# Graph kernel: block transposes on VectorE and a DMA round trip in place of TensorE transposes

## The chip, the cores and the metric

The kernel runs on one core of one Trainium2 chip. The metric is the device time of one execution in microseconds (us), lower is better. Faster or slower needs a difference of over 2%.

## The reference, cut to what matters

128 independent graphs, each with 128 nodes of 512 features and a 128x128 adjacency matrix. Everything is fp32.

```python
h = relu(layernorm(x))
H = (adj != 0);  w = adj[:, 0, :]
S = H diag(1/colsum(H)) H^T;   Dn = 1 / (H @ w)            # per graph
z = relu(Dn * S @ (h @ W1.T) + b1)                          # hidden width 1024
y = Dn * S @ (layernorm(z) * gamma + beta) @ W2.T + b2      # back to 512
x = x + (y + h)
h = relu(layernorm(x))
agg = (adj @ h) / max(rowsum(adj), 1e-6)
out = x + relu(concat(h, agg) @ W.T)
```

## The kernel before

Graphs go through a software pipeline: each step of the outer loop runs one stage of each of some fourteen graphs, and a scheduler then fixes the order in which each engine executes the instructions ("the built order" below). In the traces here an engine keeps to its order, so an instruction whose input is late holds up all behind it: in one run below, 3.78 us per graph. A tile pool hands out a fixed number of buffers in rotation (`bufs`).

A product on TensorE is written `matmul(out, a, b)` and gives the transpose of a times b, so the left operand must lie transposed. The results land in banks of a memory called PSUM, from which ScalarE or VectorE copies ("evicts") them. Four things are transposed on TensorE: two of the adjacency (`pt`), the normalised hidden layer R (`pnt`, eight 128x128 blocks) and the second layer's input h3 (`ph3`, four):

```python
    def norm_and_transposes(b):
        ...
        pt = bank("pt")
        nc.tensor.transpose(pt[:, 0:P], H.pop(b), ident)
        nc.tensor.transpose(pt[:, P : 2 * P], AN.pop(b), ident)
        ...
    def node_matrix(b):
        ps = psmall.tile([P, P + 1], FP, tag="ps_s", name="ps_s")      # one PSUM bank
        nc.tensor.matmul(ps, HT.pop(b), SB.pop(b), start=True, stop=True)
        S[b] = pool.tile([P, P], FP, tag="s", name="s", bufs=10)
        nc.scalar.activation(S[b], ps[:, :P], AF.Copy)
        dn = pool.tile([P, 1], FP, tag="dn", name="dn")
        nc.vector.tensor_copy(dn, ps[:, P : P + 1])
        ...
    def inner_transposes(b):
        n = R.pop(b)
        NT[b] = pool.tile([P, KH, P], FP, tag="nt", name="nt")
        for j in range(KH // 4):
            pt = bank("pnt")
            for i in range(4):
                k = 4 * j + i
                nc.tensor.transpose(pt[:, i * P : (i + 1) * P], n[:, k * P : (k + 1) * P], ident)
            ... # PSUM -> NT, one half by ScalarE, one by VectorE
    def conv2_weights(b):
        n = NT.pop(b)
        pg = bank("pg")
        for k in range(KH):
            nc.tensor.matmul(pg, n[:, k, :], w2[:, k, :], start=(k == 0), stop=(k == KH - 1))
        ...
    def conv2_nodes(b):
        py = bank("py")
        nc.tensor.matmul(py, S.pop(b), G.pop(b), start=True, stop=True)
        ... # VectorE evicts py into x1
```

SyncE issues three DMAs per graph: adj, x and out.

Of the kernel before, what the change touches and what calls it, by code (L numbers as in the profile page):

```python
# [8 lines left out]
FP = mybir.dt.float32  # L9
AF = mybir.ActivationFunctionType  # L10
ALU = mybir.AluOpType
AX = mybir.AxisListType
PSUM = bass.MemoryType.PSUM

# [6 lines left out]
def gnn_kernel(  # L21
# [26 lines left out]
    pool = ctx.enter_context(tc.tile_pool(name="pool", bufs=2))  # L48
    psum = ctx.enter_context(tc.tile_pool(name="psum", bufs=7, space=PSUM))
# [5 lines left out]
    X, ADJ = {}, {}  # L55

    def load(b):
        X[b] = pool.tile([P, D], FP, tag="x", name="x_t", bufs=5)
        ADJ[b] = pool.tile([P, P], FP, tag="adj", name="adj_t", bufs=4)
        nc.sync.dma_start(out=ADJ[b], in_=adj[b])  # L60
        nc.sync.dma_start(out=X[b], in_=x[b])


    row0 = const.tile([N, P], FP, name="row0")
# [6 lines left out]
    nc.scalar.dma_start(out=row0, in_=adj[:, 0, :])  # L71
    nc.scalar.dma_start(out=w1, in_=w1t.rearrange("(k p) h -> p k h", p=P))
    nc.scalar.dma_start(out=b1_bc, in_=b1.partition_broadcast(P))
    nc.gpsimd.dma_start(out=gb[:, 0, :], in_=gamma)
    nc.gpsimd.dma_start(out=gb[:, 1, :], in_=beta)
    nc.gpsimd.dma_start(out=w2, in_=w2t.rearrange("(k p) o -> p k o", p=P))
    nc.gpsimd.dma_start(out=b2_bc, in_=b2.partition_broadcast(P))
    nc.gpsimd.dma_start(out=w3, in_=wt.rearrange("(k p) o -> p k o", p=P))

    ident = const.tile([P, P], FP, name="ident")  # L80
    make_identity(nc, ident)
    eps = const.tile([P, 1], FP, name="eps")
    nc.vector.memset(eps, EPS_LN)


    wcol = const.tile([P, N], FP, name="wcol")
    pw = bank("pw")
    nc.tensor.transpose(pw[:, :N], row0, ident[:N, :N])
    nc.vector.tensor_copy(wcol, pw[:, :N])
# [37 lines left out]
    H, AN, HT, ANT, SB, S, DN = ({} for _ in range(7))  # L127
    H0, XB, Z1, R, NT, G, X1, H3, H3T, AGT = ({} for _ in range(10))

    def stats_and_incidence(b):  # L130
        ST1[b] = ln_stats(X[b], D, "l1")
        a = ADJ.pop(b)
        H[b] = pool.tile([P, P], FP, tag="h_inc", name="h_inc", bufs=3)
        nc.vector.tensor_scalar(H[b], a, 0.0, None, ALU.not_equal)
        deg = pool.tile([P, 1], FP, tag="deg", name="deg")
        nc.vector.tensor_reduce(deg, a, AX.X, ALU.add)
        rdeg = pool.tile([P, 1], FP, tag="rdeg", name="rdeg")
        nc.vector.tensor_scalar(rdeg, deg, EPS_DEG, None, ALU.max)
        nc.vector.reciprocal(rdeg, rdeg)
        AN[b] = pool.tile([P, P], FP, tag="an", name="an", bufs=3)  # L140
        nc.vector.tensor_scalar(AN[b], a, rdeg, None, ALU.mult)  # L141

    def norm_and_transposes(b):
        H0[b] = pool.tile([P, D], FP, tag="h0", name="h0", bufs=4)
        ln_relu(H0[b], X[b], *ST1.pop(b), "l1")
        pt = bank("pt")
        nc.tensor.transpose(pt[:, 0:P], H.pop(b), ident)  # L147
        nc.tensor.transpose(pt[:, P : 2 * P], AN.pop(b), ident)  # L148
        HT[b] = pool.tile([P, P], FP, tag="ht", name="ht", bufs=3)
        ANT[b] = pool.tile([P, P], FP, tag="ant", name="ant", bufs=14)  # L150
        cnt = pool.tile([P, 1], FP, tag="cnt", name="cnt")
        nc.scalar.activation(HT[b], pt[:, 0:P], AF.Copy, accum_out=cnt)
        nc.scalar.activation(ANT[b], pt[:, P : 2 * P], AF.Copy)

        be = pool.tile([P, 1], FP, tag="be", name="be")
        nc.vector.tensor_scalar(be, cnt, 1.0, None, ALU.max)
        nc.vector.reciprocal(be, be)
        SB[b] = pool.tile([P, P + 1], FP, tag="sb", name="sb", bufs=3)
        nc.vector.tensor_scalar(SB[b][:, :P], HT[b], be, None, ALU.mult)
        nc.vector.tensor_copy(SB[b][:, P : P + 1], wcol[:, b : b + 1])  # L160
        XB[b] = pool.tile([P, D], FP, tag="xb", name="xb", bufs=10)
        nc.gpsimd.tensor_tensor(XB[b], X.pop(b), H0[b], ALU.add)  # L162


    def node_matrix(b):
        ps = psmall.tile([P, P + 1], FP, tag="ps_s", name="ps_s")
        nc.tensor.matmul(ps, HT.pop(b), SB.pop(b), start=True, stop=True)  # L167
        S[b] = pool.tile([P, P], FP, tag="s", name="s", bufs=10)
        nc.scalar.activation(S[b], ps[:, :P], AF.Copy)  # L169
        dn = pool.tile([P, 1], FP, tag="dn", name="dn")  # L170
        nc.vector.tensor_copy(dn, ps[:, P : P + 1])
        inv = pool.tile([P, 1], FP, tag="inv", name="inv")
        nc.vector.tensor_scalar(inv, dn, TINY, None, ALU.max)
        nc.vector.reciprocal(inv, inv)
        DN[b] = pool.tile([P, 1], FP, tag="dinv", name="dinv", bufs=10)
        nc.vector.scalar_tensor_tensor(DN[b], dn, 0.0, inv, ALU.is_gt, ALU.mult)  # L176
# [10 lines left out]
    def conv1_weights(b):  # L187
        z = Z1.pop(b)
        R[b] = pool.tile([P, DH], FP, tag="r", name="r", bufs=5)
        for j in range(DH // 512):  # L190
            cols = slice(j * 512, (j + 1) * 512)
            po = bank("po1")
            for k in range(KD):
                nc.tensor.matmul(po, z[:, k, :], w1[:, k, cols], start=(k == 0), stop=(k == KD - 1))  # L194
            nc.vector.scalar_tensor_tensor(R[b][:, cols], po, DN[b], b1_bc[:, cols], ALU.mult, ALU.add)  # L195
        nc.scalar.activation(R[b], R[b], AF.Relu)  # L196
# [10 lines left out]
    def inner_transposes(b):  # L207
        n = R.pop(b)
        NT[b] = pool.tile([P, KH, P], FP, tag="nt", name="nt")
        for j in range(KH // 4):  # L210
            pt = bank("pnt")
            for i in range(4):
                k = 4 * j + i
                nc.tensor.transpose(pt[:, i * P : (i + 1) * P], n[:, k * P : (k + 1) * P], ident)  # L214
            dst = NT[b][:, 4 * j : 4 * j + 4, :].rearrange("p k c -> p (k c)")
            if j % 2:
                nc.scalar.activation(dst, pt, AF.Copy)  # L217
            else:
                nc.vector.tensor_copy(dst, pt)
# [18 lines left out]
    def norm_layer1(b):  # L238
        H3[b] = pool.tile([P, D], FP, tag="h3", name="h3")
        ln_relu(H3[b], X1[b], *ST3.pop(b), "l3")  # L240

    def aggregate(b):
        h, an = H3.pop(b), ANT.pop(b)
        pt = bank("ph3")
        pa = bank("pag")
        for k in range(KD):
            nc.tensor.transpose(pt[:, k * P : (k + 1) * P], h[:, k * P : (k + 1) * P], ident)  # L247
# [3 lines left out]
        H3T[b] = pool.tile([P, KD, P], FP, tag="h3t", name="h3t")  # L251
        AGT[b] = pool.tile([P, KD, P], FP, tag="agt", name="agt")
        nc.vector.tensor_copy(H3T[b].rearrange("p k c -> p (k c)"), pt)
        nc.scalar.activation(AGT[b].rearrange("p k c -> p (k c)"), pa, AF.Copy)

    def finish(b):
        halves = (H3T.pop(b), AGT.pop(b))
        po = bank("po2")
        for k in range(2 * KD):
            nc.tensor.matmul(po, halves[k // KD][:, k % KD, :], w3[:, k, :],  # L260
                             start=(k == 0), stop=(k == 2 * KD - 1))
# [15 lines left out]
        (ahead + 8, conv2_weights),  # L277
        (ahead + 9, conv2_nodes),
        (ahead + 10, norm_layer1),
        (ahead + 11, aggregate),  # L280
        (ahead + 12, finish),
# [43 lines left out]
```

## Time and profile before

| | before |
|---|---|
| time, median of 3 runs | 3257.86 us (3257.32 to 3258.47) |
| period, from one `out` to the next | 24.99 us |
| first `out` issued | 162.7 us after the start |
| DMA engines busy | 8% from 40 us on |
| SyncE | 3 DMAs per graph, 0.45 to 0.47 us each when back to back |

The view of SyncE's waits, by the line that waited and what ended the wait; the columns are us in total, times, longest:

```profile
SPq L60 <- DVE rdeg L138: 1983.2, 121, 17.4
SPq L264 <- DVE o L263: 752.5, 128, 24.6
```

SyncE stands still for over 2700 of 3256 us. L264 is the store of `out`; its 752.5 us are time in which SyncE had nothing to do but wait for a result.

### The profile page before, as it was taken

The numbers are of one execution on the slowest core, as the hardware profiler recorded it, in microseconds if no ns is written. First come the engines' busy times: TensorE is split into PE (matmuls) and PEld (weight loads), VectorE is DVE, ScalarE is ACT, GpSimd is POOL, SyncE is SP. The second block draws the span as 40 slices with busy tenths as digits, with TensorE's granted clock in tenths as the row PEclk, the third lists the DMA queues.
The fourth block names the chain that finished last, engine by engine and source line by source line (L and its number), as shares of the span: only waits on it lengthen the run. The fifth ranks groups of instructions, "written<-read, shape, count | busy, mean of one in ns | idle before, by whom it ended". The sixth has DMA issues, their size and how long they took to land.

```text
span 3256.2 us, 29056 instructions
## 1 busy us (share of the span) xinstructions
PE 3212.4 (99%) x10513; PEld 1662.9 (51%) x10513; DVE 1598.9 (49%) x4236; ACT 720.3 (22%) x1665; POOL 335.2 (10%) x267
## 2 busy tenths in 40 slices
PE   5999999999999999999999999999999999999999
PEld 2555555555555555555555555555555555555554
DVE  6644454455445544554455445544554455444332
ACT  2222222222222222222222222222222222222211
POOL 2100010011001100110010001000100010001000
PEclk9999999999999999999999999999999999999999
DMA  3000000000000000000000000000000000000000
GB/s 137 24 26 22 23 26 26 22 23 28 23 22 23 29 22 23 23 29 22 22 23 29 22 22 24 28 22 22 26 26 22 22 26 26 22 22 10 13 10 23
DMA packets 57456, 84.53 MB, mean 26 GB/s; under 512 B 6304, under 2 KB 22816, under 8 KB 57312
## 3 DMA queue, kind: packets, MB, share of 16 engines
q1 hardware_dynamic: 55296, 75.52, 7.1%
q0 software_dynamic: 1200, 4.46, 0.4%
q10 hardware_dynamic: 816, 2.69, 0.2%
q8 instruction: 82, 1.34, 0.2%
q14 instruction: 62, 0.51, 0.0%
HBM read 49.09 MB, written 33.55 MB: 25 GB/s over the span
## 4 chain that ended last, share of the span: by engine, by line
PE 98%; DMA 1%; DVE 0%; ACT 0%; SPq 0%; issue 0%; ACTq 0%
PE po L194 27%; PE po L260 27%; PE pg L225 27%; PE pz L182 4%; PE pag L249 3%; PE pnt L214 3%; PE py L233 3%; PE ph L247 2%; PE ps_s L167 1%; PE pt L147 0%; PE pt L148 0%; DMA x_t<-in_x_dram 0%; DMA adj_t<-in_adj_dram 0%; PE pc L100 0%; DVE an L141 0%; DVE rs L119 0%
## 5 line engine op out<-in xcount | busy, mean ns | idle before, releaser
L194 PE MATMUL po<-w,z 128*128 128x512 f32 x2048 | 901.4, 593 | 1.3 <-ACT z L185 1.3
L225 PE MATMUL pg<-w,nt 128*128 128x512 f32 x2048 | 899.8, 592 | 0.0
L225 PEld LDWEIGHTS pg<-w,nt 128*128 128x128 f32 x2048 | 389.0, 190 | 489.3 <-issue 475.7
L194 PEld LDWEIGHTS po<-w,z 128*128 128x128 f32 x2048 | 379.7, 190 | 431.6 <-issue 429.3
L195 DVE SCALAR_TENSOR_TENSOR r<-po,dinv,b_bc 128x512 f32<-128x512 f32 x256 | 192.2, 751 | 713.0 <-PE po L194 713.0
L260 PE MATMUL po<-w,h3t 128*128 128x512 f32 x1024 | 460.8, 593 | 0.1
L260 PE MATMUL po<-w,agt 128*128 128x512 f32 x1024 | 460.3, 592 | 0.0
L162 POOL TENSOR_TENSOR xb<-x_t,h 128x512 f32<-128x512 f32 x128 | 169.3, 1323 | 2689.0 <-ACT h L124 2689.0
L227 DVE TENSOR_TENSOR g<-pg,c 128x512 f32<-128x512 f32 x128 | 88.5, 691 | 543.6 <-PE pg L225 543.6
L196 ACT ACTIVATE r<-r 128x1024 f32<-128x1024 f32 x128 | 135.3, 1057 | 876.6 <-DVE r L195 876.6
L260 PEld LDWEIGHTS po<-w,agt 128*128 128x128 f32 x1024 | 194.6, 190 | 244.9 <-issue 244.9
L113 ACT ACTIVATE sd<-mv,eps 128x1 f32<-128x1 f32 x384 | 113.9, 298 | 837.4 <-DVE mv L111 824.7
L260 PEld LDWEIGHTS po<-w,h3t 128*128 128x128 f32 x1024 | 184.8, 190 | 185.6 <-issue 184.8
L217 ACT ACTIVATE nt<-pnt 128x512 f32<-128x512 f32 x128 | 76.4, 597 | 543.9 <-PE pnt L214 543.9
L205 DVE TENSOR_SCALAR r<-r,mv,l2rs 128x1024 f32<-128x1024 f32 x128 | 194.5, 1520 | 0.4
L182 PEld LDWEIGHTS pz<-s,h 128*128 128x128 f32 x1024 | 135.2, 193 | 61.4 <-issue 60.7
L109 DVE BATCH_NORM_STATS2 st<-r 128x6 f32<-128x512 f32 x256 | 162.8, 676 | 7.2 <-ACT r L196 7.2
L229 POOL TENSOR_TENSOR xb<-xb,b_bc 128x512 f32<-128x512 f32 x128 | 161.7, 1265 | 9.7
L214 PEld LDWEIGHTS pnt<-ident,r 128*128 128x128 f32 x1024 | 119.9, 141 | 66.9 <-issue 66.9
L176 DVE SCALAR_TENSOR_TENSOR dinv<-dn,inv 128x1 f32<-128x1 f32 x128 | 151.3, 1182 | 0.0
L235 DVE SCALAR_TENSOR_TENSOR x<-py,dinv,xb 128x512 f32<-128x512 f32 x128 | 96.1, 750 | 88.1 <-PE py L233 88.1
L182 PE MATMUL pz<-s,h 128*128 128x128 f32 x1024 | 136.0, 276 | 0.4 <-ACT s L169 0.4
(63 smaller groups left out, 2316.2 us busy)
## 6 DMA issues: line engine op xcount, KB each, us to landing
x_t<-in_x_dram SPq DMA_DIRECT2D x128, 256.0 KB, 2.7
out_dram<-o SPq DMA_DIRECT2D x128, 256.0 KB, 2.0
adj_t<-in_adj_dram SPq DMA_DIRECT2D x128, 64.0 KB, 1.8
w<-in_w1t_dram ACTq DMA_DIRECT2D x1, 2048.0 KB, 13.2
w<-in_w2t_dram POOLq DMA_DIRECT2D x1, 2048.0 KB, 15.9
w<-in_wt_dram POOLq DMA_DIRECT2D x1, 2048.0 KB, 23.3
b_bc<-in_b_dram ACTq DMA_DIRECT2D x1, 512.0 KB, 7.8
b_bc<-in_b_dram POOLq DMA_DIRECT2D x1, 256.0 KB, 16.9
```

The source lines that it names most:

```text
L109: nc.vector.bn_stats(st[:, i, :], src[:, i * 512 : (i + 1) * 512])
L162: nc.gpsimd.tensor_tensor(XB[b], X.pop(b), H0[b], ALU.add)
L176: nc.vector.scalar_tensor_tensor(DN[b], dn, 0.0, inv, ALU.is_gt, ALU.mult)
L182: nc.tensor.matmul(pz[:, k * P : (k + 1) * P], h[:, k * P : (k + 1) * P], S[b], start=True, stop=True)
L194: nc.tensor.matmul(po, z[:, k, :], w1[:, k, cols], start=(k == 0), stop=(k == KD - 1))
L195: nc.vector.scalar_tensor_tensor(R[b][:, cols], po, DN[b], b1_bc[:, cols], ALU.mult, ALU.add)
L196: nc.scalar.activation(R[b], R[b], AF.Relu)
L205: nc.vector.tensor_scalar(R[b], R[b], mv[:, 0:1], rs, ALU.subtract, ALU.mult)
L214: nc.tensor.transpose(pt[:, i * P : (i + 1) * P], n[:, k * P : (k + 1) * P], ident)
L225: nc.tensor.matmul(pg, n[:, k, :], w2[:, k, :], start=(k == 0), stop=(k == KH - 1))
L229: nc.gpsimd.tensor_tensor(XB[b], XB[b], b2_bc, ALU.add)
L260: nc.tensor.matmul(po, halves[k // KD][:, k % KD, :], w3[:, k, :], start=(k == 0), stop=(k == 2 * KD - 1))
```

## The change

Its intent is to give TensorE's transposes to engines that have time. VectorE transposes each 32x32 block in its place; the tile goes to DRAM and comes back with the blocks at their places, in runs of 32 elements, 128 B. The weights are permuted once so that their loads stay contiguous.

```diff
-        for j in range(KH // 4):
-            pt = bank("pnt")
-            ...  nc.tensor.transpose(pt[...], n[...], ident) ... copies out of PSUM
+        NT[b] = pool.tile([P, KH, P], FP, tag="nt", name="nt", bufs=3)
+        spread_blocks(NT[b], R.pop(b), DH, "n")
...
+    def spread_blocks(dst, src, width, tag):
+        K = width // P
+        t = pool.tile([P, width], FP, tag=tag + "bt", name="bt")
+        nc.vector.transpose(t, src)
+        d = dram.tile([P, width], FP, tag=tag + "d", name="scratch")
+        nc.sync.dma_start(out=d, in_=t)
+        for jj in range(Q):                      # Q = 4, B = 32
+            for i in range(Q):
+                nc.sync.dma_start(
+                    out=dst[B * jj : B * (jj + 1), :, B * i : B * (i + 1)],
+                    in_=d[B * i : B * (i + 1)].rearrange("a (j k b) -> j a k b", j=Q, k=K)[jj],
+                )
...                                              # h3 the same; adj and an by 4 DMAs each:
+    def load_blocks(dst, src):
+        for j in range(Q):
+            nc.sync.dma_start(
+                out=dst[B * j : B * (j + 1), :].rearrange("b (i a) -> b i a", a=B),
+                in_=src.rearrange("(i b) (j a) -> j b i a", b=B, a=B)[j],
+            )
...
-        S[b] = pool.tile([P, P], FP, tag="s", name="s", bufs=10)
+        S[b] = pool.tile([P, P], FP, tag="s", name="s", bufs=11)
```

More of the change, by code (lines that the diff above doesn't have):

```diff
@@ L5 @@
 from concourse import mybir
-from concourse.masks import make_identity
 from concourse._compat import with_exitstack
@@ L13 @@
 PSUM = bass.MemoryType.PSUM
+DRAM = bass.MemoryType.DRAM
 EPS_LN = 1e-5
@@ L48, in gnn_kernel @@
     pool = ctx.enter_context(tc.tile_pool(name="pool", bufs=2))
+    dram = ctx.enter_context(tc.tile_pool(name="dram", bufs=3, space=DRAM))
     psum = ctx.enter_context(tc.tile_pool(name="psum", bufs=7, space=PSUM))
@@ L53, in bank @@
         return psum.tile([P, 512], FP, tag="ps", name=name)
-    X, ADJ = {}, {}
+    X, ADJ, ADJB = {}, {}, {}
+    B = 32
+    Q = P // B
+    def load_blocks(dst, src):
[16 more added lines that the diff above has]
+                )
     def load(b):
@@ L59, in load @@
         ADJ[b] = pool.tile([P, P], FP, tag="adj", name="adj_t", bufs=4)
+        ADJB[b] = pool.tile([P, P], FP, tag="adjb", name="adjb", bufs=4)
         nc.sync.dma_start(out=ADJ[b], in_=adj[b])
+        load_blocks(ADJB[b], adj[b])
         nc.sync.dma_start(out=X[b], in_=x[b])
-    row0 = const.tile([N, P], FP, name="row0")
     w1 = const.tile([P, KD, DH], FP, name="w1")
@@ L70, in gnn_kernel @@
     gb = const.tile([P, 2, KH], FP, name="gb")
-    nc.scalar.dma_start(out=row0, in_=adj[:, 0, :])
     nc.scalar.dma_start(out=w1, in_=w1t.rearrange("(k p) h -> p k h", p=P))
     nc.scalar.dma_start(out=b1_bc, in_=b1.partition_broadcast(P))
-    nc.gpsimd.dma_start(out=gb[:, 0, :], in_=gamma)
-    nc.gpsimd.dma_start(out=gb[:, 1, :], in_=beta)
-    nc.gpsimd.dma_start(out=w2, in_=w2t.rearrange("(k p) o -> p k o", p=P))
+    for jj in range(Q):
+        part = slice(B * jj, B * (jj + 1))
+        for i, v in enumerate((gamma, beta)):
+            src = v.rearrange("(l a) (j h) -> j a h l", a=B, j=Q)[jj]
+            for h in range(2):
+                nc.gpsimd.dma_start(out=gb[part, i, 4 * h : 4 * h + 4], in_=src[:, h, :])
+        nc.gpsimd.dma_start(out=w2[part], in_=w2t.rearrange("(j k a) o -> j a k o", j=Q, a=B)[jj])
     nc.gpsimd.dma_start(out=b2_bc, in_=b2.partition_broadcast(P))
-    nc.gpsimd.dma_start(out=w3, in_=wt.rearrange("(k p) o -> p k o", p=P))
-    ident = const.tile([P, P], FP, name="ident")
-    make_identity(nc, ident)
+    for jj in range(Q):
+        nc.gpsimd.dma_start(out=w3[B * jj : B * (jj + 1), :KD, :],
+                            in_=wt[:D].rearrange("(j k a) o -> j a k o", j=Q, a=B)[jj])
+    nc.gpsimd.dma_start(out=w3[:, KD:, :], in_=wt[D:].rearrange("(k p) o -> p k o", p=P))
     eps = const.tile([P, 1], FP, name="eps")
     nc.vector.memset(eps, EPS_LN)
-    wcol = const.tile([P, N], FP, name="wcol")
-    pw = bank("pw")
-    nc.tensor.transpose(pw[:, :N], row0, ident[:N, :N])
-    nc.vector.tensor_copy(wcol, pw[:, :N])
     betas = const.tile([P, KH, P], FP, name="betas")
@@ L126, in gnn_kernel @@
     ST1, ST2, ST3 = {}, {}, {}
-    H, AN, HT, ANT, SB, S, DN = ({} for _ in range(7))
+    HT, ANB, ANT, SB, S, DN = ({} for _ in range(6))
     H0, XB, Z1, R, NT, G, X1, H3, H3T, AGT = ({} for _ in range(10))
@@ L132, in stats_and_incidence @@
         a = ADJ.pop(b)
-        H[b] = pool.tile([P, P], FP, tag="h_inc", name="h_inc", bufs=3)
-        nc.vector.tensor_scalar(H[b], a, 0.0, None, ALU.not_equal)
         deg = pool.tile([P, 1], FP, tag="deg", name="deg")
@@ L139, in stats_and_incidence @@
         nc.vector.reciprocal(rdeg, rdeg)
-        AN[b] = pool.tile([P, P], FP, tag="an", name="an", bufs=3)
-        nc.vector.tensor_scalar(AN[b], a, rdeg, None, ALU.mult)
-    def norm_and_transposes(b):
-        H0[b] = pool.tile([P, D], FP, tag="h0", name="h0", bufs=4)
-        ln_relu(H0[b], X[b], *ST1.pop(b), "l1")
-        pt = bank("pt")
-        nc.tensor.transpose(pt[:, 0:P], H.pop(b), ident)
-        nc.tensor.transpose(pt[:, P : 2 * P], AN.pop(b), ident)
+        an = pool.tile([P, P], FP, tag="an", name="an")
+        nc.vector.tensor_scalar(an, a, rdeg, None, ALU.mult)
+        d = dram.tile([P, P], FP, tag="and", name="an_scratch")
+        nc.sync.dma_start(out=d, in_=an)
+        ANB[b] = pool.tile([P, P], FP, tag="anb", name="anb")
+        load_blocks(ANB[b], d)
+        at = pool.tile([P, P], FP, tag="adjt", name="adjt")
+        nc.vector.transpose(at, ADJB.pop(b))
         HT[b] = pool.tile([P, P], FP, tag="ht", name="ht", bufs=3)
-        ANT[b] = pool.tile([P, P], FP, tag="ant", name="ant", bufs=14)
         cnt = pool.tile([P, 1], FP, tag="cnt", name="cnt")
-        nc.scalar.activation(HT[b], pt[:, 0:P], AF.Copy, accum_out=cnt)
-        nc.scalar.activation(ANT[b], pt[:, P : 2 * P], AF.Copy)
+        nc.vector.tensor_scalar(HT[b], at, 0.0, None, ALU.not_equal, ALU.add, accum_out=cnt)
         be = pool.tile([P, 1], FP, tag="be", name="be")
@@ L159, in norm_and_transposes @@
         nc.vector.tensor_scalar(SB[b][:, :P], HT[b], be, None, ALU.mult)
-        nc.vector.tensor_copy(SB[b][:, P : P + 1], wcol[:, b : b + 1])
-        XB[b] = pool.tile([P, D], FP, tag="xb", name="xb", bufs=10)
+        nc.vector.tensor_copy(SB[b][:, P : P + 1], at[:, 0:1])
+    def norm_and_transposes(b):
+        H0[b] = pool.tile([P, D], FP, tag="h0", name="h0", bufs=4)
+        ln_relu(H0[b], X[b], *ST1.pop(b), "l1")
+        ANT[b] = pool.tile([P, P], FP, tag="ant", name="ant", bufs=13)
+        nc.vector.transpose(ANT[b], ANB.pop(b))
+        XB[b] = pool.tile([P, D], FP, tag="xb", name="xb", bufs=11)
         nc.gpsimd.tensor_tensor(XB[b], X.pop(b), H0[b], ALU.add)
@@ L174, in node_matrix @@
         nc.vector.reciprocal(inv, inv)
-        DN[b] = pool.tile([P, 1], FP, tag="dinv", name="dinv", bufs=10)
+        DN[b] = pool.tile([P, 1], FP, tag="dinv", name="dinv", bufs=11)
         nc.vector.scalar_tensor_tensor(DN[b], dn, 0.0, inv, ALU.is_gt, ALU.mult)
@@ L188, in conv1_weights @@
         z = Z1.pop(b)
-        R[b] = pool.tile([P, DH], FP, tag="r", name="r", bufs=5)
+        R[b] = pool.tile([P, DH], FP, tag="r", name="r", bufs=4)
         for j in range(DH // 512):
@@ L207, in inner_transposes @@
     def inner_transposes(b):
-        n = R.pop(b)
-        NT[b] = pool.tile([P, KH, P], FP, tag="nt", name="nt")
-        for j in range(KH // 4):
-            pt = bank("pnt")
-            for i in range(4):
-                k = 4 * j + i
-                nc.tensor.transpose(pt[:, i * P : (i + 1) * P], n[:, k * P : (k + 1) * P], ident)
-            dst = NT[b][:, 4 * j : 4 * j + 4, :].rearrange("p k c -> p (k c)")
-            if j % 2:
-                nc.scalar.activation(dst, pt, AF.Copy)
-            else:
-                nc.vector.tensor_copy(dst, pt)
+        NT[b] = pool.tile([P, KH, P], FP, tag="nt", name="nt", bufs=3)
+        spread_blocks(NT[b], R.pop(b), DH, "n")
     def conv2_weights(b):
@@ L238, in norm_layer1 @@
     def norm_layer1(b):
-        H3[b] = pool.tile([P, D], FP, tag="h3", name="h3")
+        H3[b] = pool.tile([P, D], FP, tag="h3", name="h3", bufs=3)
         ln_relu(H3[b], X1[b], *ST3.pop(b), "l3")
+        H3T[b] = pool.tile([P, KD, P], FP, tag="h3t", name="h3t", bufs=4)
+        spread_blocks(H3T[b], H3[b], D, "h")
     def aggregate(b):
         h, an = H3.pop(b), ANT.pop(b)
-        pt = bank("ph3")
         pa = bank("pag")
-        for k in range(KD):
-            nc.tensor.transpose(pt[:, k * P : (k + 1) * P], h[:, k * P : (k + 1) * P], ident)
         for k in range(KD):
@@ L250, in aggregate @@
                              start=True, stop=True)
-        H3T[b] = pool.tile([P, KD, P], FP, tag="h3t", name="h3t")
         AGT[b] = pool.tile([P, KD, P], FP, tag="agt", name="agt")
-        nc.vector.tensor_copy(H3T[b].rearrange("p k c -> p (k c)"), pt)
         nc.scalar.activation(AGT[b].rearrange("p k c -> p (k c)"), pa, AF.Copy)
     def finish(b):
-        halves = (H3T.pop(b), AGT.pop(b))
+        h, g = H3T.pop(b), AGT.pop(b)
         po = bank("po2")
         for k in range(2 * KD):
-            nc.tensor.matmul(po, halves[k // KD][:, k % KD, :], w3[:, k, :],
-                             start=(k == 0), stop=(k == 2 * KD - 1))
+            lhs = h[:, k, :] if k < KD else g[:, k - KD, :]
+            nc.tensor.matmul(po, lhs, w3[:, k, :], start=(k == 0), stop=(k == 2 * KD - 1))
         o = pool.tile([P, D], FP, tag="o", name="o", bufs=3)
@@ L276, in gnn_kernel @@
         (ahead + 7, inner_transposes),
-        (ahead + 8, conv2_weights),
-        (ahead + 9, conv2_nodes),
-        (ahead + 10, norm_layer1),
-        (ahead + 11, aggregate),
-        (ahead + 12, finish),
+        (ahead + 9, conv2_weights),
+        (ahead + 10, conv2_nodes),
+        (ahead + 11, norm_layer1),
+        (ahead + 12, aggregate),
+        (ahead + 13, finish),
     ]
```

## The prediction

> **What bounds the kernel now.** I read the page first (busy shares, then the chain that ended last), then one period of the chain in order of time, then the timeline of the issuing queue and the DMA packets.
>
> ```profile
> PE 3212.4 (99%) x10513; PEld 1662.9 (51%) x10513; DVE 1598.9 (49%) x4236; ACT 720.3 (22%) x1665; POOL 335.2 (10%) x267
> ...
> PE 98%; DMA 1%; DVE 0%; ACT 0%; SPq 0%; issue 0%; ACTq 0%
> ```
>
> TensorE is busy 99% of the span and is 98% of the chain. Nothing else is above half. Busy alone would not settle it, since matmul records overlap, so I read the chain of one period, where each piece stands with its own advance:
>
> ```profile
> 1604.81 6.87 PE po L260 x16
> 1611.68 0.44 PE ph L247 x4
> 1612.12 0.89 PE pag L249 x8
> 1613.01 0.86 PE py L233 x2
> 1613.87 6.87 PE pg L225 x16
> 1620.74 0.87 PE pnt L214 x8
> 1621.61 6.87 PE po L194 x16
> 1628.48 0.89 PE pz L182 x8
> 1629.37 0.22 PE ps_s L167 x2
> 1629.59 0.11 PE pt L147
> 1629.70 0.11 PE pt L148
> 1629.81 6.87 PE po L260 x16
> ```
>
> One graph takes 1629.81 - 1604.81 = 25.00 us, all of it TensorE, with no gap between pieces. 128 graphs make 3200 us; the other 56 us of the 3256 us span are filling, draining and the one-off preparation of the second weights. In the same period VectorE is busy 12.5 us and ScalarE 5.6 us. So time is won here only by taking work from TensorE, until something else needs as long per graph.
>
> **What the Trainium skill says.** "TensorE: Matmul & The Clock Gate", Part 4: PE-mode transpose, gives about 275 ns for a 128x128 transpose in a kernel. The trace has 273 ns for one record, but four of them advance the chain by 0.44 us: 110 ns each, since they overlap. The measurement decides; the gain is counted at 110 ns, not 275.
> "VectorE: DVE Perf Modes", The three transpose paths, says that VectorE transposes 32x32 blocks only, so something else must move the blocks: here the DMA. The trace before has no such transpose.
> "DMA: Bandwidth & Descriptors", Two DMAs through the same engine are not ordered, says that a DMA which reads what another wrote must wait for its semaphore. So each read of a scratch tile stands behind the landing of its write, and the queue issues in order. The trace before has no such pair.
> The same page, Why small descriptors are slow, speaks of a fixed cost per packet. The trace agrees in kind: its packet records have a median of 9 ns for 4 B, 27 ns for 512 B, 84 ns for 2 KB and 159 ns for 4 KB, about 9 ns plus 36 ns per KB. It has no 128 B packet on this queue.
>
> **The change part by part.**
> *Removed from TensorE*, per graph: pnt 0.87, ph 0.44, the two pt 0.22, together 1.53 us. The period falls to 23.47 us; over 128 graphs 196 us, 6.0%. This is all on the path. No matmul is added.
>
> *ScalarE* loses the copies out of PSUM (0.60 + 0.28 + 0.21 + 0.29 = 1.4 us per graph). It was not the bound.
>
> *VectorE* loses two 128x512 copies (0.68 us each) and gains four transposes. An estimate from the trace's statistics instruction, which takes 694 ns for 512 fp32 elements[...], so 160 ns beside the elements: 1.23 us for 1024 elements, 0.69 for 512, 0.29 each for the two of 128. Sum +2.5 - 1.4 = +1.1 us: 13.6 of 23.5 us. It lies beside TensorE.
>
> *The issuing queue* (SyncE) goes from 3 DMAs per graph to 46: adj, 4 adjb, x, an scratch, 4 anb, h scratch, 16 h3t, n scratch, 16 nt, out. How long does an issue take? The trace has runs of back-to-back issues only at the start:
>
> ```profile
> 0.74 0.39 SPq L60 DMA_DIRECT2D adj_t<-in_adj_dram  x1
> 1.19 0.42 SPq L61 DMA_DIRECT2D x_t<-in_x_dram  x1
> 1.66 0.42 SPq L60 DMA_DIRECT2D adj_t<-in_adj_dram  x1
> 2.12 0.43 SPq L61 DMA_DIRECT2D x_t<-in_x_dram  x1
> 2.60 0.73 SPq L60 DMA_DIRECT2D adj_t<-in_adj_dram  x1
> ...
> 14.41 0.33 SPq L60 DMA_DIRECT2D adj_t<-in_adj_dram  x1
> ```
>
> A lone issue takes 0.33 us (the last line); in a run they come every 0.45 to 0.47 us. 46 x 0.47 = 21.6 us. To this comes one stall: in the built order the writes of h, n and an scratch stand together, and the first h3t read waits for the h write. A 256 KB store takes 2.0 us from issue to landing alone; behind x and out (8 packets of 84 ns per engine each, 0.67 us) it should land about 2.7 us after its issue, 1.4 us of which the two other scratch issues and the next slot cover: about 1.3 us of stall. A handful of extra waits (17 ns plus a gap of 45 ns before the issue) make 0.3. Sum: 21.6 + 1.3 + 0.3 = 23.2 us per graph, against 23.47 for TensorE. **The two are equal within my error.**
>
> *The 16 DMA engines*: adjb and anb are 512 pieces of 128 B each, h3t 2048, nt 4096, together 7168, or 448 per engine and graph. The rest per engine: x, out and h scratch 3 x 8 x 84 ns = 2.0 us; n scratch 8 x 159 = 1.3; adj and an 2 x 8 x 27 = 0.4; 46 semaphore packets of 9 ns = 0.4; sum 4.1 us. By the line above a 128 B piece is 13.6 ns, 6.1 us; if it costs as much as a 512 B one, 12.1 us. So 10 to 16 us of 23.5: hidden. It would bind at (23.47 - 4.1) / 448 = 43 ns per piece.
>
> *Latency and buffers.* At most eight of these DMAs are in flight, since each waits for the one eight before it. At 0.47 us this binds only if one takes over 3.8 us to land; adj takes 1.8. In the built order each landed tile is used about two periods after the output that let its cycle start, one stage having been added: a cycle of 20 to 24 us fits in. So I expect no wait for latency, only for throughput.
>
> *Ends.* The identity, whose making held TensorE until 30.7 us, goes away, but the last graph's tiles travel through the scratch: 2.7 us and 16 issues of 0.47, about 10 us. I leave the 56 us as they are.
>
> **The rivals.**
> 1. TensorE stays the bound: 128 x 23.47 + 56 = 3060 us, -6.0%. For it: the sums above stay below 23.47. Against: the issue sum does so by 0.3 us.
> 2. SyncE's issue becomes the bound. If a patterned DMA with 256 pieces issues in 0.52 us, as some at the start do, the sum is 46 x 0.52 + 1.6 = 25.5 us, 3320 us, +2%; at 0.60, 29.2 us, 3794 us. For it: the runs at the start show 0.73 once and 0.58 once. Against: those fell in microseconds in which the DMA engines were over 90% busy with weights, which they will not be.
> 3. The DMA engines become the bound: at 60 ns per piece 448 x 0.060 + 4.1 = 31 us, over 4000 us. For it: nothing this small has been measured here. Against: 512 B take 27 ns and a semaphore write 9.
> 4. The gain is spent on VectorE: at 13.6 of 23.5 us I see no room for this, even with transposes at twice my estimate.
>
> **Range and chances.** The floor is rival 1, 3060, or some 10 us less if the start gets shorter. A mean of the issue bound over 0.45 to 0.50 us per issue gives 22.3 to 24.6 us, and the larger of it and 23.47 averages near 24.0: 128 x 24.0 + 56 = 3128 us. The errors lie upward, as rivals 2 and 3 have no ceiling nearby. Range 3050 to 3500. Faster by over 2% needs a period below (3193 - 56) / 128 = 24.5 us: 0.52. Slower by over 2% needs one above 25.5: 0.29. Between: 0.19.
>
> **What would show each step.** Right: the page still has TensorE at 97% or more, matmul pieces without gaps, and a period of 23.5 us; VectorE near 57%; the DMA share at 45 to 70%. Rival 2: the waits of TensorE end on nt or h3t DMAs, SyncE issues without pause, every 0.5 us or more, and the DMA engines are well below full. Rival 3: the DMA share at 9 tenths in each slice, and h3t or nt reads that land 4 us or more after issue, so that the wait for the DMA eight before binds. The prediction is wrong if an issue of a 256-piece DMA takes clearly over 0.5 us, or a 128 B piece over 43 ns.

## The result, and the profile after

| | before | after |
|---|---|---|
| time, median of 4 runs | 3257.92 us | 3204.07 us (3202.39 to 3207.99) |
| period, mean of 113 steady ones | 25.00 us | 24.65 us |
| first `out` issued | 162.7 us | 182.5 us |
| DMAs issued by SyncE per graph | 3 | 46 |

The ratio is 0.9836, 95% interval 0.9819 to 0.9853: 1.6% less time. Ratios here are the mean time of one kernel's runs over that of the other's of the same rounds, so not quite the ratio of the quoted medians. The page of after, engine shares, the share of the hardware queue at the DMA engines, and the chain that ended last:

```profile
PE 3058.6 (95%) x8720; PEld 1492.6 (47%) x8720; DVE 1623.1 (51%) x4619; ACT 616.2 (19%) x1153; POOL 380.3 (12%) x286
...
q1 hardware_dynamic: 1110016, 302.37, 40.5%
...
PE 65%; SPq 17%; DMA 11%; DVE 4%; issue 3%; ACT 1%; DVEq 0%; POOL 0%
```

TensorE still looks nearly full at 95%, but its share of the chain fell from 98% to 65%. SyncE's issues (SPq) and the DMAs behind them took the rest. The DMA engines are at 40%, nowhere near full. The timeline of SyncE shows one whole cycle (start, duration, what was issued):

```profile
1614.05 0.38 SPq L277 DMA_DIRECT2D out_dram<-o  x1
1614.48 0.95 SPq L74 DMA_DIRECT2D scratch<-bt  x2
1615.48 0.53 SPq L165 DMA_DIRECT2D an_scratch<-an  x1
1619.75 7.43 SPq L77 DMA_DIRECT2D h3t<-scratch  x16
1627.28 7.78 SPq L77 DMA_DIRECT2D nt<-scratch  x16
1635.16 1.82 SPq L63 DMA_DIRECT2D anb<-an_scratch  x4
1637.02 0.43 SPq L86 DMA_DIRECT2D adj_t<-in_adj_dram  x1
1637.49 1.94 SPq L63 DMA_DIRECT2D adjb<-in_adj_dram  x4
1639.53 0.38 SPq L88 DMA_DIRECT2D x_t<-in_x_dram  x1
1640.01 0.38 SPq L277 DMA_DIRECT2D out_dram<-o  x1
```

From `out` to `out` this one takes 25.96 us (24.65 in the mean), and SyncE issues without a pause but for one hole: from 1616.01 to 1619.75, between the scratch writes and the first read of them. In the mean over the steady cycles, the step from an_scratch to the first h3t read is 2.45 us, of which about 0.49 is an ordinary step, so the stall is 2.0 us; the other 45 steps take 22.2 us, 0.493 each. The chain, in order of time (its longest pieces), goes the same way in the next cycle:

```profile
1640.10 0.28 SPq L277
1640.38 0.05 issue
1640.43 3.48 DMA scratch<-bt
1643.98 0.32 SPq L77
1644.30 0.04 issue
1644.34 0.43 SPq L77
...
1650.98 1.85 DMA h3t<-scratch
1652.84 0.09 issue
1652.93 7.11 PE po L274 x16
```

The write of h3 to the scratch lands 3.48 us after its issue. Then the h3t reads follow each other at 0.43 us plus 0.04 to 0.05 of "issue". TensorE starts on the last of them. SyncE's waits say the same:

```profile
SPq L77 <- DMA scratch<-bt: 215.4, 124, 3.7
SPq L277 <- DVE o L276: 33.0, 9, 8.7
```

The wait for the scratch write is new, in nearly every cycle. The wait for `o`, the slack, fell from 752.5 to 33.0 us. SyncE is the bound.

Where the 50 us came from, in the profiled executions: the first `out` came 19.8 us later, 113 steady periods at 24.65 instead of 25.00 us saved 39 us, and the last 14 periods, in which there is nothing left to load, saved 31 us.

### The profile page after: what moved, and what is told of

Its sections match the earlier page's. It is cut to its first block, busy times and chain, and to the rows that moved or that the text cites. A ratio compares the mean times of both kernels' runs of the same rounds, so it can differ in the third digit from the quotient of the medians. Undisturbed runs are those within 1.5% of the kernel's fastest.

```text
span 3206.2 us, 32427 instructions
## 1 busy us (share of the span) xinstructions
PE 3058.6 (95%) x8720; PEld 1492.6 (47%) x8720; DVE 1623.1 (51%) x4619; ACT 616.2 (19%) x1153; POOL 380.3 (12%) x286
## 4 chain that ended last, share of the span: by engine, by line
PE 65%; SPq 17%; DMA 11%; DVE 4%; issue 3%; ACT 1%; DVEq 0%; POOL 0%
PE po L274 25%; PE po L220 16%; PE pg L241 16%; SPq L77 14%; DMA scratch<-bt 5%; PE pag L264 3%; PE py L249 3%; DMA h3t<-scratch 2%; SPq L63 2%; PE pz L208 1%; DMA nt<-scratch 1%; DVE st L133 1%; DVE x L251 1%; DMA anb<-an_scratch 1%; PE ps_s L193 0%
## 5 line engine op out<-in xcount | busy, mean ns | idle before, releaser
L220 PEld LDWEIGHTS po<-w,z 128*128 128x128 f32 x2048 | 391.0, 191 | 497.7 <-issue 479.8
L241 PEld LDWEIGHTS pg<-w,nt 128*128 128x128 f32 x2048 | 380.1, 190 | 440.1 <-issue 438.4
L274 PE MATMUL po<-w,h3t 128*128 128x512 f32 x1024 | 475.9, 608 | 93.1 <-DMA h3t<-scratch 48.8
L276 DVE SCALAR_TENSOR_TENSOR o<-po,x 128x512 f32<-128x512 f32 x128 | 88.5, 691 | 509.6 <-PE po L274 509.6
L267 ACT ACTIVATE agt<-pag 128x512 f32<-128x512 f32 x128 | 76.4, 597 | 787.4 <-PE pag L264 787.4
L245 POOL TENSOR_TENSOR xb<-xb,b_bc 128x512 f32<-128x512 f32 x128 | 200.9, 1571 | 9.7
L72 DVE STREAM_TRANSPOSE bt<-r 128x1024 f32<-128x1024 f32 x128 | 158.0, 1235 | 32.8 <-DMA scratch<-bt 32.7
L264 PEld LDWEIGHTS pag<-ant,h 128*128 128x128 f32 x1024 | 134.4, 192 | 60.8 <-issue 60.8
L264 PE MATMUL pag<-ant,h 128*128 128x128 f32 x1024 | 134.9, 275 | 0.0
```

What stands on the lines that cost most here:

```text
L72: nc.vector.transpose(t, src)
L220: nc.tensor.matmul(po, z[:, k, :], w1[:, k, cols], start=(k == 0), stop=(k == KD - 1))
L245: nc.gpsimd.tensor_tensor(XB[b], XB[b], b2_bc, ALU.add)
L264: nc.tensor.matmul(pa[:, k * P : (k + 1) * P], h[:, k * P : (k + 1) * P], an, start=True, stop=True)
L274: nc.tensor.matmul(po, lhs, w3[:, k, :], start=(k == 0), stop=(k == 2 * KD - 1))
```

## The experiments

Theory A: SyncE's issues, about 0.49 us each, plus the stall behind the scratch write set the period. Theory B: the DMA engines or the 128 B pieces set it. Theory C: only the wait for the round trip does. Each diff is against the changed kernel unless said otherwise; ratios are against the kernel before.

### e_plus4: four more issues

```diff
         nc.sync.dma_start(out=X[b], in_=x[b])
+        for j in range(4):
+            junk = pool.tile([B, B], FP, tag="junk", name="junk", bufs=8)
+            nc.sync.dma_start(out=junk, in_=adj[b, B * j : B * (j + 1), :B])
```

> The changed kernel with four more loads per graph on SyncE, 4 KB each, into tiles that nothing reads. Theory A (SyncE's issue is the bound: 46 issues of 0.47 to 0.49 us, about 1.9 us of stall before the first h3t read and about 0.7 us of sporadic long issues make 24.65 us per graph): each issue more costs about 0.47 us in each of some 112 steady graphs, so +4 x 0.47 x 112 = +210 us, 3415 us (3380 to 3450). Theory B (the DMA engines, held up by 128 B pieces): 128 pieces more on 7168, 1.8%, at most +55 us, 3260 us. Theory C (only the landing of the scratch write before its reads counts): no change, 3205 us.

Measured 3333.11 us, ratio 1.0232 (1.0215 to 1.0249), correct. Four small loads that nobody reads cost 129 us, so issues count. In the period they cost half of what theory A said, 0.95 us of 1.88: the mean step from an_scratch to the first h3t read fell from 2.45 to 1.51 us. The h write now landed 2.35 us after its issue instead of 3.3, probably because the x load had landed before it started. The period went from 24.59 to 25.54 us in the median: 4 x 0.47 = 1.9 us of issues, less 0.94 of stall.

### e_long_runs: the same DMAs and bytes in long runs (wrong result)

```diff
+        W4 = width // Q
...
-                    out=dst[B * jj : B * (jj + 1), :, B * i : B * (i + 1)],
-                    in_=d[B * i : B * (i + 1)].rearrange("a (j k b) -> j a k b", j=Q, k=K)[jj],
+                    out=dst[B * jj : B * (jj + 1)].rearrange("a k c -> a (k c)")[:, W4 * i : W4 * (i + 1)],
+                    in_=d[B * i : B * (i + 1), W4 * jj : W4 * (jj + 1)],
```

> The changed kernel with the same number of h3t and nt reads and the same bytes, but each read takes one contiguous run per partition (1 KB for nt, 512 B for h3t) in place of 8 or 4 runs of 128 B. The result is wrong on purpose. Theory A: the number of issues is unchanged; nt issues may fall from 0.49 to 0.47 us, 16 x 0.02 = 0.3 us per graph, so 3170 us (3150 to 3205). Theory B: the pieces per graph fall from 7168 to about 2050, and the period falls to TensorE's 23.5 us, 3065 us (3050 to 3100). Theory C: no change, 3205 us, as the write's landing is the same.

Measured 3126.40 us, ratio 0.9595 (0.9581 to 0.961). The blocks land in wrong places, which was intended. The number of 128 B packets fell from 917504 to 131072, and the period only to 24.08 us: the median step of an nt read from 0.493 to 0.464 us, that of an h3t read from 0.474 to 0.464. So the short runs cost 10 to 30 ns per issue, some 0.6 us per graph, as work of the queue, and not DMA engine time. The stall stayed.

### e_split: write and reads one stage apart

```diff
-    def spread_blocks(dst, src, width, tag):
+    def write_blocks(src, width, tag, b):       # transpose and write, keep d in SCR
...
+    def read_blocks(dst, width, tag, b):        # the 16 reads of SCR.pop((tag, b))
...
         (ahead + 7, inner_transposes),
+        (ahead + 8, inner_reads),
...
         (ahead + 12, aggregate),
+        (ahead + 12, h3_reads),
```

> The scratch write and its reads stand in different stages, one stage apart, so that in the built order some 16 or more issues lie between a write and its first read. Same DMAs, same count. Theory A: only the stall of about 1.9 us per graph goes; SyncE then needs 24.65 - 1.9 = 22.8 us, below TensorE's 23.47, and TensorE binds again: 128 x 23.47 + 56 + about 25 for a longer fill = 3085 us (3055 to 3115). Theory B: unchanged, 3205 us. Theory C: like A, 3085 us; A and C are told apart by the four more issues.

Measured 3096.59 us (3092.61 to 3098.12), ratio 0.9502 (0.9487 to 0.9516), correct. The 46 DMAs are the same, but when SyncE comes to a read, its write has long landed. The chain, and SyncE's wait for `o`:

```profile
PE 94%; SPq 2%; DMA 0%; DVE 0%; issue 0%; ACT 0%; POOL 0%
```

```profile
SPq L290 <- DVE o L289: 87.5, 63, 15.9
```

TensorE is the bound again, and the period is 23.467 us in the median, as 25.00 less the removed 1.53 says. SyncE's slack is 87.5 us over 128 graphs, 0.7 us each, so it needs 22.8: 46 x 0.493 = 22.7. This version beats both kernels, by 5.0% and by 3.4% (3096.59 against 3204.07).

### e_split_plus8 and e_split_p8_pool: eight more loads, issued by SyncE or by GpSimd

```diff
 # against e_split; in e_split_p8_pool nc.gpsimd.dma_start
         nc.sync.dma_start(out=X[b], in_=x[b])
+        for j in range(8):
+            junk = pool.tile([B, B], FP, tag="junk", name="junk", bufs=8)
+            nc.sync.dma_start(out=junk, in_=adj[b, B * (j % Q) : B * (j % Q + 1), :B])
```

> The version with the writes and reads one stage apart (3097 us, period 23.47 us, SyncE with about 0.7 us of slack per graph and no stall left to absorb anything), plus eight loads per graph of 4 KB each on SyncE. Theory A (SyncE's issue): SyncE needs 22.7 + 8 x 0.47 = 26.5 us, 3.0 us over TensorE's period, in some 112 steady graphs: 3097 + 340 = 3435 us (3390 to 3480). Theory B (pieces and DMA engines) and theory C (only a stall between write and read): 3097 to 3120 us.

Measured 3512.92 us, ratio 1.0783 (1.0766 to 1.0799), correct. The chain of this run:

```profile
SPq 56%; PE 20%; DMA 9%; issue 7%; DVE 7%; ACT 1%; DVEq 0%; POOL 0%; ACTq 0%; POOLq 0%
```

54 issues, no stall, and a period of 26.79 us: 0.496 us per issue. This is the price of an issue by itself. The first `out` came at 212.5 us, against 178.0 in e_split; with the 0.3 us per period above the forecast this is most of the excess over the expectation.

> The split kernel with the same 8 extra loads per graph as the run that took 3513 us, but issued by GpSimd. Theory A (what costs is the number of issues on the one queue of SyncE, 0.47 us each): SyncE has 46 again and a slack of 0.7 us, the period stays at 23.5 us: 3097 us (3085 to 3120). Rival C (54 DMAs per graph are too many for the DMA engines or for latency, whoever issues them): 3440 to 3520 us, as with SyncE. In the built order the small TensorE product ps_s stands after py, as in the split kernel, so the order should not interfere.

Measured 3151.99 us, ratio 0.9676 (0.966 to 0.9692), correct: far below 3513, but 55 us above e_split, a miss. In the built order GpSimd issues all 1024 loads in the first 650 us, about 41 per graph instead of 8. The stretches of the timeline (PE, PEld, DVE, ACT, POOL busy, then clock, DMA share and GB/s):

```profile
380.00:440.00 60.00, 60.00 (x180) 29.84 (x179) 31.71 (x85) 12.46 (x23) 57.62 (x113) 1.00 0.52 112
500.00:560.00 60.00, 49.42 (x128) 23.58 (x127) 21.97 (x63) 8.25 (x15) 58.33 (x113) 0.89 0.39 86
```

At 380 us TensorE is busy throughout beside 41 extra DMAs per graph. From about 430 us GpSimd's own work for the graphs is late, with GpSimd full of issues, and eight periods of 26.4 to 32.1 us cost 56 us, the whole miss. Elsewhere the period is 23.5 us. So extra DMAs that SyncE does not issue leave the period alone, and theory B falls.

### e_loads_act and e_loads_pool: adj, adjb and x issued by another engine

```diff
-        nc.sync.dma_start(out=ADJ[b], in_=adj[b])
-        load_blocks(ADJB[b], adj[b])
-        nc.sync.dma_start(out=X[b], in_=x[b])
+        nc.scalar.dma_start(out=ADJ[b], in_=adj[b])     # nc.gpsimd in e_loads_pool
+        load_blocks(ADJB[b], adj[b], nc.scalar)
+        nc.scalar.dma_start(out=X[b], in_=x[b])
```

> The six loads of inputs per graph (adj, 4 adjb, x) are issued by ScalarE in place of SyncE; the DMA engines move the same pieces. Theory A: SyncE has 40 issues, 2.9 us less, and in the built order five more issues stand between the h scratch write and its reads, so most of the stall goes too: about 20.5 us, TensorE binds at 23.47: 3085 us (3055 to 3120), unless ScalarE's waits for free buffers hold up its own work. Theory B: unchanged, 3205 us. Theory C: between 3085 and 3205, as only part of the stall goes.

Measured 3250.40 us, ratio 0.9975 (0.996 to 0.999), correct: a clear miss. SyncE waited 354 us for adjb and 228 us for x, loads that ScalarE had issued, and I took the semaphores that the two hardware queues share for the cause. In that trace SyncE and ScalarE use the same eight, GpSimd's DMAs eight others.

> As the run with the six input loads on ScalarE, which came out slower than the changed kernel because SyncE's DMAs then waited for loads of ScalarE that hold the same completion semaphores. Here GpSimd issues them; in the built program its DMAs have semaphores of their own, and no DMA of SyncE waits for one of them. If that was the cause, theory A's first expectation for the loads holds now: SyncE has 40 issues, about 21.5 us with what is left of the stall, TensorE binds at 23.47: 3095 us (3070 to 3130). If another thing was the cause (the DMA engines, or the loads coming late), it stays at 3200 us or more.

Measured 3249.35 us, ratio 0.9974 (0.9958 to 0.9991), correct: the same miss without shared semaphores, so they are not what set the time. SyncE's wait for `o` is now 544.4 us, 4.4 per graph: SyncE is not the bound. The timelines of TensorE and of VectorE show what is:

```profile
1614.13 1.02 PE L249 MATMUL py<-g,s 128*128 128x512 f32 x2
1616.14 0.49 PE L193 MATMUL ps_s<-sb,ht 128*128 128x129 f32 x2 [0.99 <-DVE dn L197]
```

```profile
1615.27 0.75 DVE L251 SCALAR_TENSOR_TENSOR x<-py,dinv,xb 128x512 f32<-128x512 f32 x1 [0.25 <-PE py L249]
1615.93 0.15 DVE L197 COPY dn<-ps_s 128x1 f32<-128x1 f32 x1
```

The small product ps_s stands right behind py on TensorE. Its one PSUM bank is free only when VectorE has read dn of the graph before, and VectorE does that only after it has evicted py. So TensorE, VectorE and TensorE follow one another, 1.03 us per graph. In the changed kernel ps_s stands at the same place, but waits only for a copy that was made long before. The move of the loads let the scheduler run ps_s twelve graphs ahead of py instead of ten. It did so in e_loads_act, too, and TensorE has the same wait there, at the same median period of 24.89 us, so that wait accounts for the first miss as well. Whether the shared semaphores would cost anything without it, no run shows:

```profile
PE ps_s L193 <- DVE dn L197: 104.4, 107, 1.0
```

### e_adj_pe: the adjacency transposes back on TensorE

```diff
-        d = dram.tile([P, P], FP, tag="and", name="an_scratch")
-        nc.sync.dma_start(out=d, in_=an)
-        load_blocks(ANB[b], d)
-        nc.vector.transpose(at, ADJB.pop(b))
+        nc.tensor.transpose(pt[:, 0:P], a, ident)
+        nc.tensor.transpose(pt[:, P : 2 * P], an, ident)
+        ... # two copies out of PSUM by ScalarE; the 4 adjb loads go, too
```

> A part of the change undone: the two transposes of the adjacency per graph are on TensorE again, and the nine DMAs that replaced them (4 adjb, an scratch, 4 anb) are gone; the large transposes stay as changed, their writes and reads not split. Theory A: SyncE has 37 issues, 24.65 - 9 x 0.475 = 20.4 us plus up to 0.7 us more stall, as fewer issues stand between write and read; TensorE has 23.47 + 0.22 = 23.69 us and binds: 128 x 23.69 + 90 = 3122 us (3090 to 3140). Theory C: the stall of 1.9 us or more remains in full, so no gain over the changed kernel, 3205 us or up to 3230. Theory B: the pieces fall by 14%, 3150 us or more.

Measured 3113.33 us, ratio 0.9555 (0.9541 to 0.9569), correct. Nine issues fewer per graph give SyncE 4.4 us of slack, with 0.9 us of stall left, and the period is 23.69 us: 23.47 plus the 0.22 of the two transposes. This is the change without the part that costs nine issues for only 0.22 us of TensorE, and it keeps most of what e_split gains.

### e_split_write: short runs in the write, 28 DMAs per graph

```diff
 # against e_split
-        d = dram.tile([P, width], FP, tag=tag + "d", name="scratch")
-        nc.sync.dma_start(out=d, in_=t)
+        d = dram.tile([B, width * Q], FP, tag=tag + "d", name="scratch")
+        for i in range(Q):
+            nc.sync.dma_start(
+                out=d.rearrange("a (m i b) -> i a m b", i=Q, b=B)[i],
+                in_=t[B * i : B * (i + 1), :].rearrange("a (m b) -> a m b", b=B),
+            )
...  # and 4 contiguous reads in place of 16
```

> The split version with the 128 B runs moved to the scratch write: four writes and four reads per spread in place of one write and 16 reads, so 28 DMAs per graph in place of 46; the pieces of 128 B now are written to DRAM and the reads are contiguous. Theory A: SyncE needs about 14 us; TensorE binds at 23.47 as in the split version; only the fill and drain can get shorter, as the last graph's tiles need 8 issues in place of 17: 3085 us (3060 to 3100). If 128 B writes to DRAM are much slower than 128 B reads from it, the landing of writes shows it (over 5 us) and the time may be 3100 us or more.

Measured 3758.87 us, ratio 1.1537 (1.152 to 1.1554), correct: the largest miss. TensorE's timeline:

```profile
1618.95 1.05 PE L217 MATMUL pz<-s,h 128*128 128x128 f32 x8
1623.78 0.77 PE L202 MATMUL ps_s<-sb,ht 128*128 128x129 f32 x2 [3.78 <-DVE l2rs L239]
```

Again ps_s. In this built order it stands before the products that could fill the time, and waits for `sb` of the same period, which VectorE makes behind the statistics of R (`sb` is ready at 1623.64; the view names the next instruction, l2rs). SyncE has 1685 us of wait for `o`, so the DMAs are not at fault. The cost is larger than the 3.78 us, the period being 29.17 us. After the gap the clock that TensorE is granted is lower; in this cycle it is 0.50 of full speed in the 0.56 us of ps_s and 0.75 in the eight h3t products behind it, which take 4.55 us where the next eight take 3.44 at 1.00. The mean over the run fell to 0.937.

### e_pool_ps2 and e_sw_late_ps2: two banks for ps_s

```diff
-    psum = ctx.enter_context(tc.tile_pool(name="psum", bufs=7, space=PSUM))
-    psmall = ctx.enter_context(tc.tile_pool(name="psmall", bufs=1, space=PSUM))
+    psum = ctx.enter_context(tc.tile_pool(name="psum", bufs=6, space=PSUM))
+    psmall = ctx.enter_context(tc.tile_pool(name="psmall", bufs=2, space=PSUM))
 # e_pool_ps2: on e_loads_pool. e_sw_late_ps2: on e_split_write, and
-        (ahead + 2, node_matrix),
+        (ahead + 3, node_matrix),       # and every stage behind it one later; ht, sb: bufs=4
```

> The kernel with adj, adjb and x issued by GpSimd (3249 us, where TensorE lost 1.03 us per graph before ps_s, waiting for VectorE to read the product of the graph before out of the one PSUM bank of that pool), with two banks for ps_s and six instead of seven for the rest. Theory D (that bank wait, made by the built order, is what hid the gain): the gaps before ps_s go, the period falls from 24.9 to 23.5 to 23.7 us, 3080 to 3120 us. Rival (SyncE or the landing of the loads still binds, and the wait on VectorE only shows it): 3235 to 3260 us. If the six banks are too few, gaps appear before po1 or pz instead and the time lies between.

Measured 3245.64 us, ratio 0.9963 (0.9948 to 0.9978), correct.

> The kernel with 28 DMAs per graph and the short runs in the write (3759 us, where TensorE lost 3.8 us per graph before ps_s, waiting for sb of the same period), with ps_s one stage later and two banks for it. Theory D (only the place of ps_s in the order was at fault): no gap before ps_s, period 23.5 to 23.7 us; the extra stage lengthens the filling by up to 24 us: 3080 to 3135 us. Rival (128 B runs in a write, or so few large DMAs, are slow themselves): stays above 3300 us.

Measured 3727.66 us, ratio 1.1444 (1.1427 to 1.1461), correct. Both missed: TensorE still waited 112 us in e_pool_ps2 and 423 us in e_sw_late_ps2 before ps_s. The built order shows why. With a second bank to hand out, the scheduler ran ps_s one more graph ahead, so it waited for the same event as before. The repair had moved the instruction and left the wait.

### e_loads_pool_dn, e_dn and e_sw_late_dn: VectorE no longer reads that bank

```diff
-        S[b] = pool.tile([P, P], FP, tag="s", name="s", bufs=11)
-        nc.scalar.activation(S[b], ps[:, :P], AF.Copy)
-        dn = pool.tile([P, 1], FP, tag="dn", name="dn")
-        nc.vector.tensor_copy(dn, ps[:, P : P + 1])
+        S[b] = pool.tile([P, P + 1], FP, tag="s", name="s", bufs=11)
+        nc.scalar.activation(S[b], ps, AF.Copy)
+        dn = S[b][:, P : P + 1]
```

Applied to e_loads_pool, to the changed kernel as a control, and to e_split_write with ps_s one stage later and one bank.

> The changed kernel with adj, adjb and x issued by GpSimd (3249 us, 1.03 us per graph lost before ps_s), and ScalarE's copy of ps_s out of PSUM taking the extra column dn along, so that VectorE no longer reads that bank. In the built order ps_s now waits only for ScalarE's copy of the graph before. Theory D (the gain of the move was eaten by ps_s standing right behind py on TensorE while VectorE reads the bank only after it has evicted py): no gaps before ps_s, the period falls from 24.9 to 23.5 us, 3080 to 3115 us. Rival (38 issues on SyncE, or the loads on GpSimd, still bind): 3235 to 3260 us.

Measured 3206.73 us, ratio 0.9837 (0.9823 to 0.9852), correct. Half a miss: the wait before ps_s fell from 1.03 to 0.58 us per graph and the period from 24.88 to 24.40 us. What is left:

```profile
PE ps_s L193 <- ACT s L195: 64.7, 112, 2.7
```

ScalarE's copy of S now holds the bank, and it runs right behind py. In the built program S has eleven buffers, and the copy for one graph overwrites the S that py of eleven graphs before reads. Builds with 12 to 14 such buffers only let the scheduler run ps_s 13 to 15 graphs ahead of py instead of 12; they were not run, so that the wait would stay is argued from the order alone.

> Control: the changed kernel with only the same edit (dn copied by ScalarE together with S), all DMAs on SyncE. Theory A (SyncE's issue is the bound here, ps_s is not): nothing gained, 3195 to 3212 us against 3204. If the edit gains by itself: below 3180 us, and the last run would show nothing about the loads.

Measured 3211.90 us, ratio 0.9857 (0.9842 to 0.9872), correct. The control gains nothing, so the gain of the run before it is one of ps_s and the loads together.

> The kernel with 28 DMAs per graph and the short runs in the write (3759 us; 3728 us with ps_s one stage later and two banks, where the built order had moved ps_s up again), with ps_s one stage later, one bank, and dn copied by ScalarE. In the built order ps_s now stands behind py and waits for an sb of the period before. Theory D (the place of ps_s alone was at fault): no gap of 3.8 us, period 23.5 to 23.7 us, 3085 to 3140 us. Rival (128 B runs in a write are slow themselves): above 3300 us.

Measured 3176.34 us, ratio 0.975 (0.9734 to 0.9766), correct: 582 us less than e_split_write with the same 28 DMAs. The wait before ps_s fell to 0.37 us per graph in the steady part, the period to 24.10 us. It missed its range by 36 us because of that remaining wait, again on ScalarE's copy, but short runs in a write are cleared. That the place of ps_s explains these misses is shown as far as the gains go; no run removed what is left. But the traces show that it all lies there. Counted by starts on TensorE, from py to what follows ps_s is 1.08 us in the changed kernel and in e_split, 2.44 in e_loads_pool, 1.96 in e_loads_pool_dn and 1.72 in e_sw_late_dn. That is 1.36, 0.88 and 0.64 us more, of the 1.42, 0.93 and 0.64 us by which these three periods exceed 23.47.

## Why the prediction was right or wrong

The time fell by 54 us where 128 were forecast; the mechanism was the one named as open, and one sum was too small.

**Right: the work removed from TensorE.** With SyncE out of the way, e_split has the forecast period of 23.47 us to the hundredth (23.467).

**Right: the DMA engines.** 128 B pieces took 13 ns in the median against the estimated 13.6, and the engines were 41% busy in the steady part. Rival 3 fell, shown by e_split_p8_pool. The forecast share of 45 to 70% was slightly high.

**Right: VectorE and ScalarE lie beside.** The two large transposes took 1235 and 704 ns against estimates of 1.23 and 0.69 us, those of 128 elements 310 instead of 290. The 160 ns beside the elements rested on a rate that the trace before does not give; these sizes give 1.04 ns per element and some 175 ns beside. VectorE was busy 12.7 us per graph rather than 13.6; two instructions that the sum left alone became shorter (`dinv` 174 ns instead of 1182, the normalisation of R 965 instead of 1520), for a reason that no run shows. It did not bind in either kernel.

**Wrong: "Sum: 21.6 + 1.3 + 0.3 = 23.2 us per graph".** The mean cycle measured 24.65 us. Two terms were too small. The stall was 2.0 us instead of 1.3, as the write of h landed 3.3 us after its issue in the median and not 2.7. Here the sum itself was wrong: it names two transfers ahead of the write, x and out, but adds the 0.67 us of one; 2.0 + 2 x 0.67 is 3.3. The issues took 46 x 0.493 = 22.7 us instead of 21.9 with the extra waits: an nt read takes 0.493 us in the median and not 0.47, 0.35 us for fifteen, and about once in a cycle an issue or the pause behind it lasts 0.2 to 1.5 us longer, 0.7 us in the mean; a few other steps were a little shorter than 0.47. I had seen such long ones at the start (0.73 and 0.58) and put them down to the weights. That reading was not safe: from 2 to 3 us the DMA engines were busy 92%, but 68% with SyncE's own adj and x, and from 3 to 3.5 us 77%. The cause stays open.

**Wrong with it: the average over the maximum.** The period was taken as 24.0 us, from issues of 0.45 to 0.50 us. Measured was 24.65, at the top of that range. 128 x 0.65 = 83 us, less 5 us since the ends took 51 and not 56 (3206.2 - 128 x 24.65), is the 78 us between the forecast and the profiled execution.

**Rival 2 came true, by another way.** SyncE became the bound, but not through issues of 0.52 us or more for patterned DMAs: e_long_runs puts the whole pattern at 0.6 us per graph. Nor did the latency of eight DMAs in flight bind: SyncE's waits for landings other than those of the h and n writes sum to 24 us. What bound was the plain number of issues plus one wait in the order, and e_split shows that removing the wait alone is enough to give the bound back to TensorE.

**The signs I named.** TensorE at 97% and no gaps would have been rival 1; the trace had 95%, 93 us of gaps before the h3t products, and SyncE issuing without a pause. The DMA share well below full told rivals 2 and 3 apart at once, as the text said it would. The sign named for being wrong, an issue of a 256-piece DMA clearly over 0.5 us, did not come (0.493 in the median): the sum failed on the stall and on many small excesses.

## What to carry to other kernels

When work moves to DMAs, count the issues per period and multiply by the step measured in that queue, not by the duration of a lone one, then add every wait that stands in the queue's order: here 46 steps fitted beside TensorE and one wait of 2 us did not. Put a stage between a write to DRAM and its reads before you look for fewer or longer DMAs. When an edit moves instructions to another queue, read the built order of the engine that should profit: moving the loads off SyncE lost its gain, and rewriting the scratch ended 15% above the kernel before, on a product of 0.2 us that had come to stand in front of its input.

## What the Trainium skill lacked or had wrong

- "DMA: Bandwidth & Descriptors", Issuing engines are not separate DMA queues, calls the sequencer's time to initiate a DMA usually small relative to the DMA itself, and this section gives no figure per issue; the page's table of `DmaMemcpy` costs has 512 cycles of the sequencer per instruction for earlier generations, and no time. Here it was the bound: 0.493 us of SyncE per issue (0.464 in the median for contiguous reads, 0.493 for 256 pieces of 128 B), 22.7 us per graph, while the DMA engines were 41% busy.
- The same page, Why small descriptors are slow, gives a fixed cost in cycles and no duration for a 128 B piece. The runs show 13 ns in the median, against 27 ns for 512 B: twice as dear per byte, not more.
- "VectorE: DVE Perf Modes", The three transpose paths, has one duration, for bf16. For fp32 the runs show 310 ns for 128x128, 704 for 128x512 and 1235 for 128x1024.
- "TensorE: Matmul & The Clock Gate", Part 4, gives the duration of one transpose in a kernel, 275 ns. The trace agrees (273 ns), but what counted was the step of 110 ns, and the gain of e_split agrees with it.
- No page that I read says that freeing a queue can change the scheduler's order on another engine: 1.03 us per graph before ps_s in e_loads_pool, 3.78 in e_split_write.
